# A graph network on one core: the first group of columns in two passes, with only the first part of its edges counted ahead

## Chip, cores, metric

The kernel runs on one core of a Trainium2 chip. The metric is device time in microseconds (us) of one execution; lower is better.

## The reference

A graph with N = 2500 nodes and E = 80000 edges, sorted by destination; 256 features; three layers.

```python
h = jnp.maximum(_layernorm(x), 0.0)
xs = [h]
for W, b in ((W0, b0), (W1, b1), (W2, b2)):        # W is 512 x 256
    xi, xj = h[dst], h[src]
    m = jnp.concatenate([xi, xj - xi], axis=-1) @ W + b
    s   = jax.ops.segment_sum(m, dst, num_segments=N)
    cnt = jax.ops.segment_sum(ones, dst, num_segments=N)
    h = jax.nn.relu(s / jnp.maximum(cnt, 1.0)[:, None])
    xs.append(h)
out = x + jnp.concatenate(xs, axis=-1) @ Wf + bf
```

The sum over a node's edges is a product with a matrix of counts: A[m, n] is the number of edges from m to n. Each layer multiplies node features (already times W) by A, and adds an "own" term from the node's features times its degree.

## The kernel before

**Names.** `P` = 128 partitions; `NT` = 20 tiles of 128 nodes; `DC` = 2 halves of the 256 features; `W` = 6 nodes in a window; `BW` = 4 windows in a block, which is 24 columns of A; `TURN` = 3 blocks. The columns of A are cut into 5 groups: four of 84 windows (504 columns, 21 blocks each) and one of 81 windows (486 columns). Blocks are numbered through: 0 to 20 are group 0, 21 to 41 group 1, and so on.

**Queues.** PE multiplies, DVE does elementwise work on one side, ACT on the other; POOL and SP mostly start transfers. The prefix `o` (`PEo`, `ACTo`, ...) means that instructions stay in the order in which the program writes them. Each engine takes its own in that order and waits on the others by semaphores. All such calls go through one helper, so they all have line 282 in the profile; there, they are told apart by tile names.

**Building A.** Three steps make a block b of A:

- `compare(b)`, on DVE: one-hot tiles `one_m` (source within its tile) and `one_n` (window position and tile). One call serves two blocks (15 with 16, 17 with 18, ...), except blocks 0 and 41, which stand alone. There are three buffers of each tile, so a compare waits until the blocks of three pairs earlier are counted.
- `counts(b)`, on PE: 8 small bf16 matmuls of `one_n` by `one_m` into a bank of PSUM.
- `take_counts(b, a)`, on ACT: a copy of that bank into the columns of tile `a` (20 tiles of rows by 504).

`build(g, a)` does this for a group in turns of three blocks and compares four blocks ahead. `degrees(i)` gets in-degrees: 8 sums on ACT (`junk`), three steps on DVE (`deg`, `deg_b`), four empty steps, then two sets of 6 small matmuls with a copy into `cnt`. `finish(g, a)` puts the degrees into a spare row of `a` and writes `a` out to `a_dram` in four transfers by POOL; for group 0, POOL's additions of x to `acc` follow.

**Head.** Normalizing x, finding edges, turning features, the products with W and Wf, and blocks of group 0 are woven together in an order written out by hand (the string `order`). In it, B is `compare`, C `counts`, E `take_counts`, with the block's number. Z and F are products (PE, tile `pz`, by W and by Wf, one pair q of tiles each); H and L split a Z product into a high and a low part (`zh` on ACT, `zl` on DVE); G copies an F product to `acc` on ACT. T and R turn features (PE, then ACT). `ws` is a subtraction on the own weights (`wt`) on DVE. The products have four banks of PSUM, and each is free for the next product, or after the head for something else, when H and L, or G, have read it. The head ends with all 21 blocks of group 0 counted and blocks up to 24 compared.

**Layer 0.** A loop goes over the five groups. `layer(l, g, a, own)` multiplies `zh` and `zl` with the group's columns, as a generator that yields after each unit. A unit is one row tile k: four matmuls (two feature halves, high and low) of 504 columns. Four further units are the own products (f32, tile `wt` by `hT`). After each unit the loop may step the next group's `build` (at the places in `at`) and an `extra` generator. For group 0, `extra` is

```python
extra = chain(degrees(0), finish(0, a), later_loads(), degrees(1))
```

stepped one and a half times a unit. `by_count(g)` multiplies `hT` with the degrees on DVE, ahead of the group's own units. So while group 0's columns are multiplied, group 1's blocks are counted.

**Rest.** Layers 1 and 2 read A back from `a_dram`, and use a fast form of the product on pairs of groups; the tail writes the result out.

Of the kernel before, what the change touches and what calls it, by code (L numbers as in the profile page):

```python
# [8 lines left out]
F32 = mybir.dt.float32  # L9
I32 = mybir.dt.int32  # L10
AF = mybir.ActivationFunctionType
# [296 lines left out]
def chain(*its):  # L308
    for it in its:
        yield from it  # L310
# [3 lines left out]
def by_windows(ctx: ExitStack, tc: tile.TileContext, x, src, dst, Ws, bs, Wf, bf, out, missing):  # L314
    nc = tc.nc
    PE, DVE, ACT, POOL, SP = nc.tensor, nc.vector, nc.scalar, nc.gpsimd, nc.sync
    PEo, DVEo, POOLo, ACTo, SPo = (InOrder(tc, e) for e in (PE, DVE, POOL, ACT, SP))
    P = 128
    N, D = x.shape
    E = src.shape[0]  # L320
    NT = (N + P - 1) // P
# [3 lines left out]
    DC = D // P  # L325
    R = E // P
    W = 6
# [10 lines left out]
    BW = 4  # L338
# [33 lines left out]
    def bank():  # L372
        return ps[-1].tile([P, 512], F32, name="bank")
# [10 lines left out]
    cnt = early.tile([P, NP], BF16, name="cnt")  # L384
# [29 lines left out]
    def tile_of(z, t):  # L414
        return z[:, t % 2, t // 2 * D:(t // 2 + 1) * D]
# [20 lines left out]
    ws = [None] * L  # L436
# [198 lines left out]
    def degrees(i):  # L635

        for q in range(W + 2):
            junk = hot.tile([P, CAP], BF16, name="junk2")
            ACTo.activation(junk, away[:, i, :], AF.Relu, bias=nc_[:, q:q + 1], accum_out=gsum[:, i, q:q + 1])
            yield  # L640
        DVEo.scalar_tensor_tensor(deg[:, i, :], gsum[:, i, 1:W + 1], -2.0, gsum[:, i, 0:W], op0=OP.mult, op1=OP.add)
        DVEo.tensor_add(deg[:, i, :], deg[:, i, :], gsum[:, i, 2:W + 2])
        DVEo.tensor_copy(deg_b[:, i, :], deg[:, i, :])
        yield
        yield
        yield
        yield
        for w0 in range(0, min(P, NW - i * P), P // 2):
            n = min(P // 2, NW - i * P - w0)
            pc = bank()  # L650
            for c in range(W):
                PEo.matmul(pc[:, :n * W].rearrange("p (w c) -> p w c", c=W)[:, :, c],
                          deg_b[:, i, c:c + 1].to_broadcast([P, P]), ident_b[:, w0:w0 + n], start=True, stop=True)
            to = (i * P + w0) * W
            ACTo.copy(cnt[:, to:to + n * W], pc[:, :n * W])
            yield
# [110 lines left out]
    def group_of(g):  # L767
        return sum(GWS[:g]) * W, GWS[g] * W
# [5 lines left out]
    def new_a(g):  # L774
        return apools[g % 2].tile([P, NT, GS], F32R, name="a")

    windows = [(g, s, min(BW, GWS[g] - s)) for g in range(NG) for s in range(0, GWS[g], BW)]
# [34 lines left out]
    def take_counts(b, a):  # L812
        _, s, nb = windows[b]
        ACTo.copy(
            a[:, :, s * W:(s + nb) * W].rearrange("p t (w c) -> p t w c", c=W),
            counted.pop(b)[:, :nb * NB].rearrange("p (w c t) -> p t w c", w=nb, c=W))

    def build(g, a):

        bs = [b for b in range(len(windows)) if windows[b][0] == g]  # L820
        for i in range(0, len(bs), TURN):
            for b in bs[i:i + TURN]:
                counts(b)
            for b in bs[i:i + TURN]:
                take_counts(b, a)
            for b in bs[i:i + TURN]:
                compare(b + AHEAD)
            yield

    def finish(g, a):  # L830
        c0, n = group_of(g)
        if n < GS:
            DVEo.memset(a[:, :, n:].bitcast(F32), 0.0)
        ACTo.copy(a[PAD:PAD + 1, NT - 1, :n], cnt[PAD:PAD + 1, c0:c0 + n])
        for t in range(0, NT, 5):
            POOLo.dma_start(a_dram[g][:, t:t + 5, :], a[:, t:t + 5, :].bitcast(F32))
        if g == 0:
            for t in range(0, NT, 5):
                add_x(t, t + 5)
        yield  # L840
# [6 lines left out]

    unit = [None]

    def layer(l, g, a, own, PE=PE, ACT=ACT):  # L850

        c0, n = group_of(g)
        pa = [ps_left.tile([P, 512], F32, name="bank") for _ in range(DC)]
        ways = [(o, c) for o in range(DC) for c in range(DC)]
        units = [(0, k) for k in BY_TURNS]
        for i, u in enumerate(own):
            units.insert(u + i, (1, i))
        last = {}
        for kind, i in units:
            last.update({o: (kind, i, o) for o in (range(DC) if kind == 0 else ways[i][:1])})  # L860
        for kind, i in units:
            if kind == 0:
                for o in range(DC):
                    for z in (zh, zl):
                        unit[0] = PE.matmul(pa[o][:, :n], tile_of(z, i)[:, o * P:(o + 1) * P], a[:, i, :n],
                                            start=(i == 0 and z is zh),
                                            stop=(z is zl and last[o] == (kind, i, o)))
            else:
                o, c = ways[i]
                unit[0] = PE.matmul(pa[o][:, :n], ws[l][0][:, c, o * P:(o + 1) * P], hT[:, c, c0:c0 + n],  # L870
                                    start=False, stop=(last[o] == (kind, i, o)))
            yield
        for o in range(DC):
            ACT.activation(hT[:, o, c0:c0 + n], pa[o][:, :n], AF.Relu)

# [3 lines left out]

    groups = [(0, 1), (1, 2), (2, 4), (4, 6), (6, 8), (8, Q)]
    a = new_a(0)
    acts = {
        "lim": limits, "first": find_first, "next": find_next, "pick": find_rows,
        "long": lengthen,
        "dstr": lambda: ACTo.copy(dst_r[:, MORE:], dst_i),
# [13 lines left out]
        long warm8 lim io first next dstr st0 rs0 sq0 pick sc0 warm7 N0 pk00 sg00 pk01 st1 T0 pk11 R0 sg01 st4 rs1 sq1 Z0 pk30 se0  # L901
        sg11 sc1 pk20 N1 st5 sg30 ge0 T1 st6 R1 rs3 F0 sg20 pk21 sq3 st7 pk10 H0 F1 rs4 st3 sq4 sc4 G0 st9
        sc3 L0 sg21 N6 pk31 ka0 kb0 Z1 N5 st8 N7 G1 T6 rs5 sg10 sg31 km0 T5 se1 kt0 R6 H1 st2 F6 sq5 sc5 k10 k20
        rs2 Z6 ge1 L1 T7 B0 R5 R7 Z5 B1 C0 B2 ka1 G6 H6 N9 H5 C1 T9 F7 E0 ge2 kb1 R9 sq2 km1 E1 kt1 C2 B3 k21 Z9
        k11 N8 L6 B4 E2 L5 C3 B5 C4 T8 E3 E4 C5 V9 R8 E5 ge3 ka2 H9 sc2 Z7 H7 F8 G7 B6 N3 N2 ka3 km2 T2 R2 km3
        kb2 C6 T3 kb3 B7 L7 kt2 Z2 B8 B9 L9 E6 C7 k22 k12 kt3 H2 N4 E7 B10 k13 k23 Z8 L2 C8 T4 C9 E8
        C10 H8 E9
        F9 B11 B12 C11 G8 E10 C12 R4 E12 E11 B13 F5 B14 C13 R3 B15 C14 E13 E14 L8 B16 Z3 G9 B17 C15 C16 H3 E15
        G5 B18 F3 C17 E16 C18 F4 E17 B19 C19 Z4 L3 G3 B20 E18 C20 B21 F2 E19 B22 H4 E20 L4 G4 B23 G2 B24 ws
    """  # L910

    def perform(order):
# [7 lines left out]
    ps_left = banks_of.enter_context(tc.tile_pool(name="ps_left", bufs=4, space=PSUM))  # L920
# [7 lines left out]
    def later_loads():  # L928
        load_wb(1, SPo)
        load_wt(1, SPo)  # L930
        load_wf(1, SPo)
        SPo.dma_start(bf_sb, bass.AP(tensor=bf.tensor, offset=bf.offset, ap=[[0, P], [1, D]]))
        yield
# [6 lines left out]
    E12 = 4096.0  # L940
    C1 = 1.0 + 1.0 / E12
# [61 lines left out]
            DVEo.tensor_add(acc[:, t:t + 5, :], acc[:, t:t + 5, :], bf_sb.unsqueeze(1).to_broadcast([P, 5, D]))  # L1003
            yield

    LATE = [NT] * 4
    extra = chain(degrees(0), finish(0, a), later_loads(), degrees(1))
    for g in range(NG):
        at = {}
        own = LATE  # L1010
        if g + 1 < NG:
            a1 = new_a(g + 1)
            one = build(g + 1, a1)
            left = -(-len([b for b in windows if b[0] == g + 1]) // TURN)
            units = NT + DC * DC
            at = {(i + 1) * (units - 1) // left - 1 for i in range(left)}
            if g:
                own = [u + 1 - i for i, u in enumerate(sorted(at)[1:5])]
        else:
            second.close()  # L1020
            ready = ctx.enter_context(tc.tile_pool(name="ready", bufs=7, side="right"))
            extra = chain(shares(), first_forms())
        for u, _ in enumerate(layer(0, g, a, own, PEo, ACTo)):
            if u in at:
                next(one)
            next(extra, None)
            if g == 0 and u % 2:
                next(extra, None)
            if g == 0 and u == NT // 2 + 3:
                by_count(0)  # L1030
            if u == NT - 1 and g + 1 < NG:
                run(extra)
                by_count(g + 1)
        run(extra)
        if g + 1 < NG:
            run(finish(g + 1, a1))
            a = a1
        extra = chain(degrees(g + 2) if g + 2 < WG else ())
# [261 lines left out]
    for l in range(1, L):  # L1300
# [7 lines left out]
        for i in range(Q + LAG):  # L1308
            if 0 < i <= Q:
                lone.make(i - 1)  # L1310
            if i < Q:
                q = order[i]
                n = Nodes(l, q)
# [51 lines left out]
    for i, q in enumerate(order):  # L1365
        po = bank()
        po = [po[:, :D], bank()[:, :D] if i == Q - 1 else po[:, D:]]
        for k in range(2):
            if q in PLAIN:
                for c in range(DC):  # L1370
                    PEo.matmul(po[k], hT[:, c, (2 * q + k) * P:(2 * q + k + 1) * P], wfs[L][:, c, :],
                               start=(c == 0), stop=(c == DC - 1))
            else:
                times(po[k], splits[q], k, coming[0])
        for k in range(2):
            t = 2 * q + k
            add_to_acc(t, po[k])
            n = P if t < NT - 1 else LAST
# [42 lines left out]
```

## Time and profile before

| | |
|---|---|
| median of 3 runs | 478.6 us (478.38 to 479.85) |
| profiled execution | 478.51 us |
| its span, first to last instruction | 476.7 us |
| mean granted TensorE clock | 0.996 |
| layer 0, group 0 on PE | 61.9 to 93.4 us of the span |
| PE busy / DVE busy / ACT busy | 465.9 / 375.0 / 302.1 us |

Times in the profile are counted from the span's start; the profiled execution takes 1.8 us more than its span. PE is the matmuls, PEld the loads of their weights. In a timeline, a row gives the start, the time, engine, line, operation, names out<-in, shapes and count, and in brackets the idle time ahead of it and what ended it. Consecutive instructions of a kind are merged. Ends of matmuls are modelled, so spacings are best taken from starts. The chain of waits is followed back from the last instruction to whatever released each one.

### The profile page before, as it was taken

To read this page: it belongs to the slowest core of one execution; us is meant where nothing else is said; L and a number is where in the kernel's file an instruction comes from. 1 tells how busy PE (TensorE), PEld (TensorE's weight loads), DVE (VectorE), ACT (ScalarE), POOL (GpSimd) and SP (SyncE) were. 2 spreads that over 40 slices of the span, in tenths; PEclk is the share of its full clock that TensorE was granted. 3 is DMA by queue.
4 is the path that set the end of the run, shared out by engine and by line. 5 is a ranking of instruction groups with operands and counts; after the bars stand their busy time and mean duration, and the time that the engine had idled before them with its cause. 6 is when DMAs were issued, how large, how long until landed. Compare 5 with 4: busy or idle time off the path is not lost.

```text
span 476.7 us, 7301 instructions
## 1 busy us (share of the span) xinstructions
PE 465.9 (98%) x2723; PEld 366.5 (77%) x2723; DVE 375.0 (79%) x687; ACT 302.1 (63%) x527; POOL 41.6 (9%) x66
## 2 busy tenths in 40 slices
PE   7999999999999999999999999999999999999994
PEld 4887888777777778878887877876788788688694
DVE  8988987987788874649987847877899687569785
ACT  5776576664554435067778866874787798497540
POOL 3681015200100101000000000000000000000000
PEclk9999999999999999999999999999999999999998
DMA  9310078990550905522268551110213955220033
GB/s 285 112 53 4 1 156 162 192 214 9 102 118 1 203 16 101 119 89 52 79 188 321 210 174 27 61 43 2 87 43 90 356 185 175 87 88 0 0 98 124
DMA packets 21845, 52.73 MB, mean 111 GB/s; under 512 B 1977, under 2 KB 12170, under 8 KB 21770
## 3 DMA queue, kind: packets, MB, share of 16 engines
q1 hardware_dynamic: 14730, 34.31, 21.2%
q0 software_dynamic: 5856, 16.51, 18.2%
q10 hardware_dynamic: 1216, 1.37, 0.9%
q8 instruction: 23, 0.38, 0.3%
q14 instruction: 20, 0.16, 0.1%
HBM read 36.72 MB, written 16.10 MB: 111 GB/s over the span
## 4 chain that ended last, share of the span: by engine, by line
PE 87%; DVE 7%; DMA 2%; POOL 2%; issue 1%; SPq 0%; DVEq 0%
PE bank L282 85%; PE pz L282 2%; DMA acc<-in_x_dram 1%; DVE st L282 1%; DVE acc L282 1%; POOL acc L282 1%; DVE one_m L282 1%; DVE staged L282 1%; DMA es<-longer,start_i 1%; POOL ed L282 1%; DVE one_n L282 1%; DVE zl L282 0%; DVE away L282 0%; DVE mv L282 0%; POOL es L282 0%
## 5 line engine op out<-in xcount | busy, mean ns | idle before, releaser
L282 ACT CAST block<-staged 128x1008 fp32r<-128x1008 bf16 x120 | 117.8, 1031 | 16.9 <-DVE staged L282 6.3
L282 ACT CAST a<-bank 128x480 fp32r<-128x480 f32 (+1 forms) x105 | 52.9, 565 | 60.7 <-PE bank L282 60.7
L282 PE MATMUL bank<-a,zh 128*128 128x504 f32 (+1 forms) x200 | 84.4, 422 | 0.0
L282 PE MATMUL bank<-block,zh 128*128 128x504 f32 (+1 forms) x200 | 83.8, 419 | 0.0
L282 DVE TENSOR_TENSOR one_m<-iota_m,key_m 128x2048 bf16<-128x2048 bf16 (+2 forms) x55 | 64.3, 1169 | 21.4 <-PE bank L282 21.3
L282 PE MATMUL bank<-a,zl 128*128 128x504 f32 (+1 forms) x200 | 77.9, 389 | 0.0
L282 PE MATMUL bank<-block,zl 128*128 128x504 f32 (+1 forms) x200 | 77.4, 387 | 0.0
L282 PE MATMUL bank<-block,sh 128*128 128x504 f32 x160 | 69.1, 432 | 0.0
L282 PE MATMUL bank<-block,staged 128*128 128x512 f32 (+1 forms) x312 | 66.5, 365 | 0.3 <-DVE staged L282 0.3
L282 PE MATMUL bank<-block,sl 128*128 128x504 f32 x160 | 62.7, 392 | 0.0
L282 PEld LDWEIGHTS bank<-block,staged 128*128 128x128 f32 x312 | 52.5, 188 | 10.7 <-issue 0.7
L282 DVE TENSOR_TENSOR one_n<-iota_n,key_n 128x960 bf16<-128x960 bf16 (+2 forms) x110 | 55.5, 545 | 0.0
L282 DVE TENSOR_TENSOR block<-staged 128x1008 fp32r<-128x1008 bf16 x40 | 46.9, 1205 | 5.5 <-PE bank L282 4.3
L282 PEld LDWEIGHTS <-one_m 128*128 128x128 bf16 x834 | 39.1, 98 | 11.2 <-issue 7.2
L282 PEld LDWEIGHTS bank<-a,zh 128*128 128x128 f32 x200 | 37.8, 189 | 10.7 <-issue 2.6
L282 PEld LDWEIGHTS bank<-block,zh 128*128 128x128 f32 x200 | 37.6, 188 | 10.8 <-issue 2.5
L282 PEld LDWEIGHTS bank<-block,zl 128*128 128x128 f32 x200 | 37.6, 188 | 10.5 <-issue 3.2
L282 PE MATMUL bank<-one_n,one_m 128*128 128x120 bf16 x834 | 44.5, 209 | 1.1 <-DVE one_n L282 1.0
L282 PEld LDWEIGHTS bank<-a,zl 128*128 128x128 f32 x200 | 37.8, 189 | 8.9 <-issue 2.6
L282 DVE TENSOR_TENSOR staged<-staged 128x1008 bf16<-128x1008 bf16 x40 | 27.1, 679 | 17.3 <-ACT block L282 16.9
L282 PE MATMUL pz<-wbf,hT 128*128 128x256 f32 x160 | 38.6, 387 | 0.7 <-DMA wbf<-in_L_gnn_Wf_dram 0.4
L282 PEld LDWEIGHTS bank<-block,sh 128*128 128x128 f32 x160 | 30.1, 188 | 10.4 <-issue 3.5
(155 smaller groups left out, 591.1 us busy)
## 6 DMA issues: line engine op xcount, KB each, us to landing
staged<-a_dram SPq DMA_DIRECT2D x52, 504.0 KB, 4.0
a_dram<-a POOLq DMA_DIRECT2D x20, 630.0 KB, 8.6
out_dram<-acc SPq DMA_DIRECT2D x17, 128.0 KB, 1.8
acc<-in_x_dram POOLq DMA_DIRECT2D x3, 640.0 KB, 13.1
wbf<-in_L_gnn_Wf_dram SPq DMA_DIRECT2D x4, 256.0 KB, 6.9
acc<-in_x_dram SPq DMA_DIRECT2D x1, 896.0 KB, 9.4
acc<-in_x_dram ACTq DMA_DIRECT2D x1, 768.0 KB, 6.9
wbf<-in_L_gnn_W_dram SPq DMA_DIRECT2D x3, 256.0 KB
```

Source lines behind the costliest of these rows:

```text
L282: return self.tc.keep_in_program_order(call(*args, **kwargs))
```

## The change

Group 0 is multiplied in two passes: first its columns 0 to 263 (blocks 0 to 10), then columns 264 to 503 (blocks 11 to 20).

- The head counts blocks 0 to 10 only, and compares up to 14. Ten counts, ten copies and five pairs of compares leave it. Ten steps of `degrees(0)` come into it (D in the order): the 8 sums on ACT, the DVE steps, one empty step.
- `layer` takes `cuts`. With one cut it has two spans, each with its own two banks of PSUM (four in all), its own 80 matmuls (264 or 240 columns) and its own pair of final activations.
- During the first pass, after units 0, 5, 10 and 15, blocks 11 to 20 are counted, copied and the next ones compared. During the second pass, after units 20, 23, 26, 30, 33, 36 and 40, group 1's blocks are.
- The own units of the first span stand in the second pass (from unit 28), those of the second at its end. There are thus 8 of half the width instead of 4.
- `extra` is stepped once a unit. The first span's part of the degree row is written in the first pass, the rest and the transfers of `finish` after unit 20.

```diff
+    def with_degrees(a, c0, x0, x1):
+        ACTo.copy(a[PAD:PAD + 1, NT - 1, x0:x1], cnt[PAD:PAD + 1, c0 + x0:c0 + x1])
     def finish(g, a):
...
-        ACTo.copy(a[PAD:PAD + 1, NT - 1, :n], cnt[PAD:PAD + 1, c0:c0 + n])
+        with_degrees(a, c0, 0 if g else HALF * BW * W, n)
...
-    def layer(l, g, a, own, PE=PE, ACT=ACT):
+    def layer(l, g, a, own, PE=PE, ACT=ACT, cuts=()):
         c0, n = group_of(g)
-        pa = [ps_left.tile([P, 512], F32, name="bank") for _ in range(DC)]
+        ends = [0, *cuts, n]
+        spans = list(zip(ends, ends[1:]))
+        pa = {(s, o): ps_left.tile([P, 512], F32, name="bank")[:, :s[1] - s[0]] for s in spans for o in range(DC)}
         ways = [(o, c) for o in range(DC) for c in range(DC)]
-        units = [(0, k) for k in BY_TURNS]
-        for i, u in enumerate(own):
-            units.insert(u + i, (1, i))
+        units = [(s, k, None) for s in spans for k in BY_TURNS]
+        for i, (u, s) in enumerate(own):
+            units.insert(u + i, (spans[s], None, ways[i % len(ways)]))
...
-                        unit[0] = PE.matmul(pa[o][:, :n], tile_of(z, i)[:, o * P:(o + 1) * P], a[:, i, :n],
+                        unit[0] = PE.matmul(pa[s, o], tile_of(z, k)[:, o * P:(o + 1) * P], a[:, k, s[0]:s[1]],
...
+            if ending[s] == (k, way):
+                for o in range(DC):
+                    ACT.activation(hT[:, o, c0 + s[0]:c0 + s[1]], pa[s, o], AF.Relu)
             yield
...
-        C10 H8 E9
-        F9 B11 B12 C11 G8 E10 C12 R4 E12 E11 B13 F5 B14 C13 R3 B15 C14 E13 E14 L8 B16 Z3 G9 B17 C15 C16 H3 E15
-        G5 B18 F3 C17 E16 C18 F4 E17 B19 C19 Z4 L3 G3 B20 E18 C20 B21 F2 E19 B22 H4 E20 L4 G4 B23 G2 B24 ws
+        C10 H8 E9
+        F9 B11 D B12 G8 E10 R4 B13 F5 B14 R3 L8 Z3 G9 H3 D
+        G5 F3 F4 Z4 L3 G3 F2 H4 L4 G4 G2 ws
...
-    LATE = [NT] * 4
-    extra = chain(degrees(0), finish(0, a), later_loads(), degrees(1))
+    def second_half(a):
+        yield from build(0, a, HALF)
+        built.append(0)
+    def when_built():
+        with_degrees(a, 0, 0, HALF * BW * W)
+        while not built:
+            yield
+    HALF = 11
+    extra = chain(early_degrees, when_built(), finish(0, a), later_loads(), degrees(1))
...
+        passes = 1 if g else 2
+        own = [(NT + 8, 0)] * 4 + [(NT * 2, 1)] * 4 if g == 0 else [(NT, 0)] * 4
...
+            if g == 0:
+                one = chain(second_half(a), one)
+                at = {0, 5, 10, 15} | {NT + u - 2 for u in at}
...
-        for u, _ in enumerate(layer(0, g, a, own, PEo, ACTo)):
+        for u, _ in enumerate(layer(0, g, a, own, PEo, ACTo, () if g else (HALF * BW * W,))):
             if u in at:
                 next(one)
             next(extra, None)
-            if g == 0 and u % 2:
-                next(extra, None)
-            if g == 0 and u == NT // 2 + 3:
+            if g == 0 and u == NT + 2:
                 by_count(0)
-            if u == NT - 1 and g + 1 < NG:
+            if u == NT * passes - 1 and g + 1 < NG:
                 run(extra)
                 by_count(g + 1)
```

More of the change, by code (lines that the diff above doesn't have):

```diff
@@ L816, in take_counts, with build @@
             counted.pop(b)[:, :nb * NB].rearrange("p (w c t) -> p t w c", w=nb, c=W))
-    def build(g, a):
-        bs = [b for b in range(len(windows)) if windows[b][0] == g]
+    def build(g, a, start=0):
+        bs = [b for b in range(len(windows)) if windows[b][0] == g][start:]
         for i in range(0, len(bs), TURN):
@@ L858, in layer @@
         last = {}
[L859 to L862, printed above, removed]
+        ending = {}
+        for s, k, way in units:
+            ending[s] = k, way
+            last.update({(s, o): (k, way) for o in (range(DC) if way is None else way[:1])})
+        for s, k, way in units:
+            if way is None:
                 for o in range(DC):
                     for z in (zh, zl):
-                        unit[0] = PE.matmul(pa[o][:, :n], tile_of(z, i)[:, o * P:(o + 1) * P], a[:, i, :n],
-                                            start=(i == 0 and z is zh),
-                                            stop=(z is zl and last[o] == (kind, i, o)))
-            else:
-                o, c = ways[i]
-                unit[0] = PE.matmul(pa[o][:, :n], ws[l][0][:, c, o * P:(o + 1) * P], hT[:, c, c0:c0 + n],
-                                    start=False, stop=(last[o] == (kind, i, o)))
+                        unit[0] = PE.matmul(pa[s, o], tile_of(z, k)[:, o * P:(o + 1) * P], a[:, k, s[0]:s[1]],
+                                            start=(k == 0 and z is zh), stop=(z is zl and last[s, o] == (k, None)))
+            else:
+                o, c = way
+                unit[0] = PE.matmul(pa[s, o], ws[l][0][:, c, o * P:(o + 1) * P], hT[:, c, c0 + s[0]:c0 + s[1]],
+                                    start=False, stop=(last[s, o] == (None, way)))
+            if ending[s] == (k, way):
+                for o in range(DC):
+                    ACT.activation(hT[:, o, c0 + s[0]:c0 + s[1]], pa[s, o], AF.Relu)
@@ L872, in layer @@
             yield
-        for o in range(DC):
-            ACT.activation(hT[:, o, c0:c0 + n], pa[o][:, :n], AF.Relu)
     groups = [(0, 1), (1, 2), (2, 4), (4, 6), (6, 8), (8, Q)]
     a = new_a(0)
+    early_degrees = degrees(0)
     acts = {
+        "D": lambda: next(early_degrees),
         "lim": limits, "first": find_first, "next": find_next, "pick": find_rows,
@@ L903, in by_windows @@
         sc3 L0 sg21 N6 pk31 ka0 kb0 Z1 N5 st8 N7 G1 T6 rs5 sg10 sg31 km0 T5 se1 kt0 R6 H1 st2 F6 sq5 sc5 k10 k20
-        rs2 Z6 ge1 L1 T7 B0 R5 R7 Z5 B1 C0 B2 ka1 G6 H6 N9 H5 C1 T9 F7 E0 ge2 kb1 R9 sq2 km1 E1 kt1 C2 B3 k21 Z9
-        k11 N8 L6 B4 E2 L5 C3 B5 C4 T8 E3 E4 C5 V9 R8 E5 ge3 ka2 H9 sc2 Z7 H7 F8 G7 B6 N3 N2 ka3 km2 T2 R2 km3
-        kb2 C6 T3 kb3 B7 L7 kt2 Z2 B8 B9 L9 E6 C7 k22 k12 kt3 H2 N4 E7 B10 k13 k23 Z8 L2 C8 T4 C9 E8
+        rs2 Z6 ge1 L1 T7 B0 R5 R7 Z5 B1 C0 B2 ka1 G6 H6 N9 H5 C1 T9 F7 E0 D ge2 kb1 R9 sq2 km1 E1 D kt1 C2 B3 k21 Z9
+        k11 N8 L6 B4 E2 D L5 C3 B5 C4 T8 E3 D E4 C5 V9 R8 E5 D ge3 ka2 H9 sc2 Z7 H7 F8 G7 B6 N3 N2 ka3 km2 T2 R2 km3
+        kb2 C6 T3 kb3 B7 L7 kt2 Z2 B8 B9 L9 E6 D C7 k22 k12 kt3 H2 N4 E7 D B10 k13 k23 Z8 L2 C8 T4 C9 E8 D
         C10 H8 E9
-        F9 B11 B12 C11 G8 E10 C12 R4 E12 E11 B13 F5 B14 C13 R3 B15 C14 E13 E14 L8 B16 Z3 G9 B17 C15 C16 H3 E15
-        G5 B18 F3 C17 E16 C18 F4 E17 B19 C19 Z4 L3 G3 B20 E18 C20 B21 F2 E19 B22 H4 E20 L4 G4 B23 G2 B24 ws
+        F9 B11 D B12 G8 E10 R4 B13 F5 B14 R3 L8 Z3 G9 H3 D
+        G5 F3 F4 Z4 L3 G3 F2 H4 L4 G4 G2 ws
     """
@@ L1004, in first_forms @@
             yield
-    LATE = [NT] * 4
-    extra = chain(degrees(0), finish(0, a), later_loads(), degrees(1))
+    built = []
+    def second_half(a):
[7 more added lines that the diff above has]
+    extra = chain(early_degrees, when_built(), finish(0, a), later_loads(), degrees(1))
     for g in range(NG):
         at = {}
-        own = LATE
+        passes = 1 if g else 2
+        own = [(NT + 8, 0)] * 4 + [(NT * 2, 1)] * 4 if g == 0 else [(NT, 0)] * 4
         if g + 1 < NG:
@@ L1016, in by_windows @@
             at = {(i + 1) * (units - 1) // left - 1 for i in range(left)}
+            if g == 0:
+                one = chain(second_half(a), one)
+                at = {0, 5, 10, 15} | {NT + u - 2 for u in at}
             if g:
-                own = [u + 1 - i for i, u in enumerate(sorted(at)[1:5])]
+                own = [(u + 1 - i, 0) for i, u in enumerate(sorted(at)[1:5])]
         else:
```

## The prediction

> **What bounds the kernel now.** I read the page first, then the chain of waits, then the stretches around the end of the head, then timelines. The page gives the engine, the chain says from when on.
>
> ```profile
> PE 465.9 (98%) x2723; PEld 366.5 (77%) x2723; DVE 375.0 (79%) x687; ACT 302.1 (63%) x527; POOL 41.6 (9%) x66
> PE 87%; DVE 7%; DMA 2%; POOL 2%; issue 1%; SPq 0%; DVEq 0%
> ```
>
> ```profile
> 47.26 0.49 DVE one_n L282
> 47.75 0.04 issue
> 47.80 0.81 PE bank L282 x15
> 48.61 1.80 PE pz L282 x8
> 50.41 0.71 PE bank L282 x16
> ...
> 60.45 1.80 PE pz L282 x8
> 62.25 400.54 PE bank L282 x2258
> ```
>
> The last piece of the chain that is not PE's, until the tail, is a compare ending at 47.75 us: block 11 waits for its one_n. From there PE is the chain for 415 us. So the stretch from which the change takes work (47.5 to 61.9) and the one into which it puts work (61.9 to 93.4, layer 0 of group 0) have the same bound:
>
> ```profile
> core 0: us, PE busy (x) PEld busy (x) DVE busy (x) ACT busy (x) POOL busy (x), PEclk, DMA share, GB/s
> 47.48:61.90 14.42, 14.32 (x129) 12.55 (x129) 13.14 (x20) 8.84 (x18) 0.42 (x1) 1.00 0.01 1
> 61.90:93.37 31.47, 31.47 (x283) 24.49 (x281) 26.89 (x46) 21.32 (x60) 8.69 (x9) 1.00 1.00 181
> ```
>
> A busy PE may hide slack, so I checked by start times: between 47.48 and 61.90 stand ten count blocks of 0.355 us (3.55) and six products of 1.80 (10.8), 14.35 in all. It is full except for block 11's wait, 0.26 us.
>
> **What the Trainium skill says.** "TensorE: Matmul & The Clock Gate", Back-to-back issue gap: the isolated gap is N/2.4 + 2.5 ns, and in a stream the weight load also sets the spacing. Halving a matmul would thus cost some 2.5 ns each. The trace spaces 504 columns by 0.228 us, above the formula's 212 ns; I use the trace. Same page, LDWEIGHTS: 128 columns take about P/1.2, 107 ns, whatever the row count. A 240-column matmul at 1/2.4 ns per column is 100 ns, so its load is barely covered. The trace has the nearest case in its tail (256 columns, new weights each time, 119 ns). "VectorE: DVE Perf Modes", perf-mode tier table: a bf16 tensor_tensor of 2048 takes 1224 ns; one_m takes 1.22 us here, so compares have nothing to gain. "Perfetto Trace Analysis", Identifying the Most-Contended Engine: matmul busy share is a bad measure of headroom; hence the sums by start times.
>
> **The prices**, in the PE timeline:
>
> ```profile
> 64.37 0.40 PE L282 MATMUL bank<-a,zh 128*128 128x504 f32 x1
> 64.60 0.39 PE L282 MATMUL bank<-a,zl 128*128 128x504 f32 x1
> 64.84 1.24 PE L282 MATMUL bank<-one_n,one_m 128*128 128x120 bf16 x24
> 65.90 0.48 PE L282 MATMUL bank<-a,zh 128*128 128x504 f32 x1
> 66.22 0.39 PE L282 MATMUL bank<-a,zl 128*128 128x504 f32 x1
> ...
> 455.18 5.87 PE L282 MATMUL bank<-block,staged 128*128 128x256 f32 x48
> 460.89 0.38 PE L282 MATMUL bank<-wbf,hT 128*128 128x256 f32 x1
> ```
>
> Read starts, not durations: 64.60 - 64.37 gives 0.228 us for 504 columns; a turn of three blocks takes 1.06; the first matmul after a turn takes 0.32, 0.09 over the rest. The 256-column run is (460.89 - 455.18)/48 = 0.119 us. A line through 0.228 and 0.119 has 0.44 ns a column and 6 ns fixed.
>
> **The change, step by step (PE).**
> 1. Removed from the head: blocks 11 to 20. By starts they take 0.97 (11, 12, with the wait) + 3 x 0.71 + 2 x 0.355 = **-3.81 us**. The six products among them stay, now back to back.
> 2. Added in the first pass: the same ten blocks, 10 x 0.355 = **+3.55**, in four turns, each followed by the slower first matmul, 4 x 0.09 = **+0.36**.
> 3. 80 matmuls of 504 columns become 160 of 264 and 240: 80 x 6 ns = **+0.5**. Bounds: -1.4 if one column costs 1/2.4 ns and nothing else (160 x 105 against 80 x 228 ns), +1.4 if the whole 18 ns over 210 is fixed. The middle is the trace's own 256-column row. The 8 own passes in f32 become 16 of half width; 256 columns take 0.225 and 504 take 0.445, so nothing.
> 4. A new wait. Block 11's bank now comes from the banks that the head's products held, one unit (0.49 us) into the layer, and in the changed program its matmul waits for the copy of the last product F2 (G2 on ACT). Before, no block came until three units were done.
>
> ```profile
> 62.29 0.59 ACT L282 COPY acc<-pz 128x512 f32<-128x512 f32 x1 [0.62 <-PE pz L282]
> ```
>
> That copy ends 0.98 us after the layer's first matmul; block 11 would start at 0.49. **+0.45** (0 to 0.6). Behind it in PE's order stands the whole first pass.
>
> **The change on DVE.** Five pairs of blocks (15/16 to 23/24) leave the head: 5 x 2.11 us (starts 64.06, 66.17) = 10.6. They aren't free time gained: DVE then waits in the head for L8, L3, L4, which follow the products, and can't run ahead, since the pairs stand behind L4 and "ws" in its order.
>
> ```profile
> 60.75 0.69 DVE L282 TENSOR_TENSOR zl<-pz,zh 128x512 fp32r<-128x512 f32 x1 [1.28 <-ACT zh L282]
> 63.46 0.68 DVE L282 TENSOR_TENSOR wt<-wt,wbf 128x512 f32<-128x512 f32 x1
> 64.06 1.22 DVE L282 TENSOR_TENSOR one_m<-iota_m,key_m 128x2048 bf16<-128x2048 bf16 x1
> ...
> 69.30 1.23 DVE L282 TENSOR_TENSOR one_m<-iota_m,key_m 128x2048 bf16<-128x2048 bf16 x1 [0.94 <-PE bank L282]
> ...
> 78.72 1.23 DVE L282 TENSOR_TENSOR one_m<-iota_m,key_m 128x2048 bf16<-128x2048 bf16 x1 [2.47 <-PE bank L282]
> 80.83 1.27 DVE L282 TENSOR_TENSOR hT<-hT,cnt 128x504 f32<-128x504 f32 x2
> ```
>
> Those gaps at 69.30 and 78.72 (and 0.89 at 92.19) are all the slack DVE had in the layer: 31.47 - 26.89 = 4.6 us. I laid both orders side by side from the layer's start T. DVE: L4 ends at T - 0.35, "ws" at T + 0.3, then pairs of 2.11, each held until the blocks of three pairs earlier are counted. Pair 15 ends at 2.4, 17 at 4.5, 19 at 7.9 (waits for block 14), 21 at 10, 23 at 12, 25 at 15.1 (block 20), 27 at 18.3 (block 22); then by_count(0), 1.2; 29 at 21.6; 31 at 23.7; 33 at 25.8; 35 at 27.9; deg 0.55; 37 at 30.6; 39 at 32.7; 41 (single, 1.1) at 33.8. PE, with steps 2 to 4, asks for block 19 at 9.7, 25 at 18.2, 29 at 21.1 (**0.5 late**), 31 at 24.2, 33 at 26.4, 35 at 27.1 (**0.8 late**), 37 at 30.9, 39 at 33.5, 41 at 34.2. So **+1.3** of DVE waits in the second pass (0 to 3: each margin is under 1.5 us, and one late pair delays all behind it).
>
> **What else moves.** Eight degree sums go to the head, 8 x 0.5 on ACT. ACT idles 6 us between 31 and 45, the sums follow E's, and the queue is caught up at H7 (35.55) and H2 (41.06): nothing for PE. After E8 it runs 0.5 late; H8, G8, R4, R3 have 0.7 or more before their products. The three deg steps on DVE push pair 13 and L8 by 0.5: L8 ends at about 50.95 and F3, which takes that bank, starts at 51.08. Nothing, but tight (0 to 0.3). POOL's 4 a_dram writes and the additions of x, and SP's four later loads, keep their order and are issued at T + 17 = 75 us, against 76.7 before: nothing, since group 2's first copy comes 20 us later. Four accumulation banks instead of two: the first pass's are emptied in the second, before group 1 needs them: nothing. In group 1 DVE is ahead again (block 42 asked 4 us after its pair).
>
> **Sum.** -3.81 + 3.55 + 0.36 + 0.5 + 0.45 + 1.3 = **+2.3 us**. Head ends at about 58.1, group 0's layer at 95.7 instead of 93.4. Profiled execution 478.51 (span 476.7 and 1.8 around it), 0.1 under the median 478.6; so 480.8 against the former, and **480.9** as a median. About 0.3% (1.4 us) can be told from no change.
>
> **Rivals.**
> - A. As summed, PE work moved and small waits added: 479.8 to 482.6. For it: a full PE on both sides. Chance 0.62.
> - B. DVE becomes the bound of group 0's layer. 13 pairs, one single, 42/43, both by_counts and deg are 34 us, plus 2.9 of buffer waits, in a layer PE needs 36 for; should each of the last eight pairs come 0.4 later (say, a late "ws"), +3.2: 484. Chance 0.15.
> - C. The change costs PE only its sums (no late pair, no bank wait): +0.6, 479.2. For it: margins that I may have taken too tight. Chance 0.15.
> - D. Faster: PE takes short matmuls and their loads without overhead. A column costs 1/2.4 ns and nothing else (-1.4 in step 3), the slower first matmul after a turn is gone (step 2 at 3.55), and no wait comes: -3.81 + 3.55 - 1.4 = -1.7, 476.9. It decides once a 264-column matmul is spaced under some 113 ns; the 256-column row (119) speaks against it. Chance 0.08. That the head's DVE-bound part gets shorter is excluded: all that PE waits for before block 11 (0.38 at 32.85, 0.35 at 38.96, 0.30 at 41.33) stays where it is.
>
> Range 478.8 to 484.0: it leaves out most of D, the edge of C and the far end of B. Faster 0.07 (D), same 0.18 (C and A's lower edge), slower 0.75.
>
> **What the changed profile would show.** Layer 0's first 264-column matmul at 58.1 (58 to 58.6). Spacing of 264 and 240 columns: 0.122 and 0.112 us. PE idle at block 11 put down to ACT's acc copy. Blocks 29 and 35 waiting for one_n. DVE with 10 us more in that layer and gaps of a few us in the head. First matmul of group 1 at 95.7. I am wrong if group 1 starts before 93 us, or if PE shows no wait in the second pass.

## The result, and the profile after

The change makes the kernel slower by about 2 us: 480.73 us (median of 6 runs, 480.34 to 481.79) against 478.8 for the kernel before (6 runs, 478.38 to 479.85), ratio 1.0041 [1.0031, 1.0052]. The profiled execution took 480.81 us, with a span of 479.0 us at a granted clock of 0.996. The forecast was 480.9.

The busy line of the changed kernel's page, and the shares of its chain by engine:

```profile
PE 466.7 (97%) x2811; PEld 372.7 (78%) x2811; DVE 374.8 (78%) x687; ACT 302.5 (63%) x530; POOL 41.6 (9%) x66
PE 86%; DVE 7%; DMA 3%; POOL 2%; issue 1%; ACT 0%; SPq 0%; DVEq 0%
```

There are 88 more matmuls (80 from the two passes, 8 from the own units). PE is busy 0.8 us longer in a span 2.3 us longer, so most of the loss is not work. The chain of waits shows where PE no longer carries it:

```profile
45.81 12.39 PE pz L282 x56
...
58.23 0.59 ACT acc L282
...
58.87 15.23 PE bank L282 x188
...
79.53 1.22 DVE one_m L282
...
83.82 1.14 DVE one_m L282
84.96 0.98 DVE one_n L282 x2
...
85.98 378.92 PE bank L282 x2093
```

Before, PE was the chain from 47.80 us on. Now an ACT copy stands in it at 58.23, and DVE's one-hots stand in it in the second pass. The same stretches as before, cut at the new end of the head:

```profile
core 0: us, PE busy (x) PEld busy (x) DVE busy (x) ACT busy (x) POOL busy (x), PEclk, DMA share, GB/s
45.65:57.84 12.19, 12.19 (x60) 10.47 (x58) 6.58 (x13) 6.16 (x13) 0.00 (x0) 1.00 0.00 0
57.84:95.41 37.57, 36.45 (x451) 34.82 (x449) 34.54 (x54) 23.27 (x57) 10.47 (x12) 1.00 0.75 138
```

The head ends 4.06 us earlier than before (57.84 against 61.90). The layer takes 37.57 us instead of 31.47, which is 6.10 more. So group 1 starts 2.04 us later (95.41 against 93.37), and that is nearly all of the 2.3 us in the span. In the layer, PE stands idle 1.12 us between its instructions; before, it showed no idle time there. DVE is busy 34.5 us of 37.6, where it was 26.9 of 31.5. PE's timeline in the layer (start, time, engine, line, operation, count, and in brackets the idle time ahead and what ended it):

```profile
57.84 0.47 PE L282 MATMUL bank<-a,zh 128*128 128x264 f32 x1
...
58.87 1.22 PE L282 MATMUL bank<-one_n,one_m 128*128 128x120 bf16 x24 [0.19 <-ACT acc L282]
...
70.94 0.28 PE L282 MATMUL bank<-a,zl 128*128 128x264 f32 x1
...
72.63 0.28 PE L282 MATMUL bank<-a,zl 128*128 128x264 f32 x1
...
74.46 0.28 PE L282 MATMUL bank<-a,zl 128*128 128x240 f32 x1
...
75.58 0.28 PE L282 MATMUL bank<-a,zl 128*128 128x240 f32 x1
...
79.27 0.23 PE L282 MATMUL bank<-one_n,one_m 128*128 128x120 bf16 x1 [0.19 <-DVE one_n L282]
79.66 0.46 PE L282 MATMUL bank<-one_n,one_m 128*128 128x80 bf16 x7 [0.17 <-DVE one_n L282]
...
85.58 0.23 PE L282 MATMUL bank<-one_n,one_m 128*128 128x120 bf16 x1 [0.41 <-DVE one_n L282]
85.98 0.46 PE L282 MATMUL bank<-one_n,one_m 128*128 128x80 bf16 x7 [0.17 <-DVE one_n L282]
...
95.41 0.57 PE L282 MATMUL bank<-a,zh 128*128 128x504 f32 x1
```

Starts tell more than the brackets, since the modelled end of the matmul ahead covers part of each wait. Against the spacing without a wait, block 11 starts 0.35 us late, block 29 (79.27 and 79.66) is late by 0.69 and block 35 by 0.90, together **1.94 us**. From 70.94 to 72.63 are 14 matmuls of 264 columns, 0.121 us each; from 74.46 to 75.58 ten of 240, 0.112 each. And DVE in the same layer:

```profile
57.12 0.69 DVE L282 TENSOR_TENSOR zl<-pz,zh 128x512 fp32r<-128x512 f32 x1 [4.71 <-ACT zh L282]
...
63.80 1.23 DVE L282 TENSOR_TENSOR one_m<-iota_m,key_m 128x2048 bf16<-128x2048 bf16 x1 [1.17 <-PE bank L282]
...
70.95 1.22 DVE L282 TENSOR_TENSOR one_m<-iota_m,key_m 128x2048 bf16<-128x2048 bf16 x1 [0.74 <-PE bank L282]
...
74.12 1.23 DVE L282 TENSOR_TENSOR one_m<-iota_m,key_m 128x2048 bf16<-128x2048 bf16 x1 [0.98 <-PE bank L282]
...
76.23 1.27 DVE L282 TENSOR_TENSOR hT<-hT,cnt 128x504 f32<-128x504 f32 x2
```

DVE has nothing to do for 4.71 us at the end of the head. It then waits 2.89 us for free buffers: 1.91 in the first pass, and 0.98 at the start of the second, which begins at 72.75. Then it does `by_count(0)` (76.23) ahead of the one-hots that PE needs next. Up to 74.12 DVE waits for PE; from 78.9 on PE waits for DVE.

### The profile page after: what moved, and what is told of

It reads as the page before. It is cut to its first block, busy times and chain, and to the rows that moved or that the text cites. A ratio compares the mean times of both kernels' runs of the same rounds, so it can differ in the third digit from the quotient of the medians.

```text
span 479.0 us, 7483 instructions
## 1 busy us (share of the span) xinstructions
PE 466.7 (97%) x2811; PEld 372.7 (78%) x2811; DVE 374.8 (78%) x687; ACT 302.5 (63%) x530; POOL 41.6 (9%) x66
## 4 chain that ended last, share of the span: by engine, by line
PE 86%; DVE 7%; DMA 3%; POOL 2%; issue 1%; ACT 0%; SPq 0%; DVEq 0%
PE bank L282 83%; PE pz L282 3%; DMA acc<-in_x_dram 1%; DVE one_m L282 1%; DVE one_n L282 1%; DVE acc L282 1%; DMA es<-in_src_dram,start_i 1%; POOL acc L282 1%; DVE staged L282 1%; POOL ed L282 1%; DMA es<-longer,start_i 1%; DVE st L282 1%; POOL es L282 0%; DVE away L282 0%; DVE kn L282 0%
## 5 line engine op out<-in xcount | busy, mean ns | idle before, releaser
L282 PE MATMUL bank<-a,zh 128*128 128x504 f32 (+3 forms) x240 | 89.0, 383 | 0.0
L282 PE MATMUL bank<-a,zl 128*128 128x504 f32 (+3 forms) x240 | 81.6, 352 | 0.0
L282 PEld LDWEIGHTS bank<-a,zh 128*128 128x128 f32 x240 | 45.4, 189 | 8.7 <-issue 2.6
L282 PEld LDWEIGHTS bank<-a,zl 128*128 128x128 f32 x240 | 45.3, 189 | 7.7 <-issue 2.6
L282 PEld LDWEIGHTS bank<-block,zh 128*128 128x128 f32 x200 | 37.6, 188 | 10.8 <-issue 2.5
L282 PEld LDWEIGHTS bank<-block,zl 128*128 128x128 f32 x200 | 37.6, 188 | 10.6 <-issue 3.2
L282 PE MATMUL pz<-wbf,hT 128*128 128x256 f32 x160 | 37.4, 384 | 0.8 <-DMA wbf<-in_L_gnn_Wf_dram 0.5
```

What stands on the lines that cost most here:

```text
L282: return self.tc.keep_in_program_order(call(*args, **kwargs))
```

## Experiments

All ratios are to the kernel before, run beside each experiment on the same chip (478.56, 478.79 and 478.91 us in the three sets of runs). The head in the order of before ended at 61.64, 61.90, 62.02 and 62.16 us in four traces, so a single start is read to about 0.5 us, and lengths within a stretch more finely. The head of the changed kernel ended at 57.84 to 57.87 in four traces. From group 1's first matmul to the end of the span the traces take 383.3 to 384.4 us, except for that of `two_passes_five_groups`, which changes the later groups too; so the spans of two single traces say little below 1 us. Medians and the layer's own length say more.

### The split of the matmuls alone

`two_passes_alone` is the kernel before with only the layer of group 0 in two passes. All 21 blocks are still counted in the head, and group 1's turns stand at the doubled places. The basis of the three kernels of this part, on the changed one:

```diff
-    HALF = 11
+    HALF, CUT = 21, 264
...
-    extra = chain(early_degrees, when_built(), finish(0, a), later_loads(), degrees(1))
+    extra = chain(degrees(0), when_built(), finish(0, a), later_loads(), degrees(1))
...
-                at = {0, 5, 10, 15} | {NT + u - 2 for u in at}
+                at = {2 * u for u in at}
```

and the order of the head is that of the kernel before (`CUT` also takes the place of the old cut where the degree row is written and where `layer` is called).

> The head is that of before (all 21 blocks counted, compares up to 24); only layer 0 of group 0 runs in two passes of 264 and 240 columns, group 1's turns spread over both. Theory A (the forecast's sum: PE is full on both sides, so the moved blocks cancel and what is left is the price of short matmuls, turns and new waits): PE pays only the split, 0.4 us by the changed kernel's spacings (80 x 0.1207 + 80 x 0.1117 against 80 x 0.228): 0.1 to 0.8 us over before, PE without a wait in the layer. Rival S (the split itself is the whole loss, for instance by loads of weights that are no longer covered): 1.5 to 2.5 us over before.

Measured: 479.49 us, ratio 1.0018 [1.0010, 1.0025], +0.9 us. The layer runs from 61.64 to 93.78, 32.14 us, +0.67 on the kernel before. Two causes stand out. The spacings give 80 x (0.121 + 0.112 - 0.228) = +0.4. The other is one wait, in which the degree matmuls of group 1 come before DVE has their sums (idle before them in PE's timeline):

```profile
81.40 0.51 PE L282 MATMUL bank<-ident_b,deg_b 128*128 128x64 bf16 x6 [0.27 <-DVE deg_b L282]
```

The bracket has 0.27 us; by starts this matmul is 0.44 late (0.66 after the one ahead, where 0.22 is usual), so the other small changes of order give back some 0.2. The split itself is what theory A said, and the expectation missed a wait that the rearrangement brought. The rival's 18 ns for each matmul is out.

`two_passes_five_groups` does the same for all five groups (`passes = 2`, the cut passed for each).

> As two_passes_alone, but all five groups of layer 0 run in two passes (264 and 240 columns; the last 264 and 222). It multiplies the price of the split by five. Theory A: 5 x 0.4 to 0.5 = 2.0 to 2.5 us over before. Rival S: 7 us or more. If a bank of PSUM is waited for at the change of groups, PE shows it as a wait for ACT.

Measured: 481.46 us, ratio 1.0059 [1.0045, 1.0073], +2.8 us. That is above A's range and far under the rival's. The reason is the last group: its 486 columns become 264 and 222, and the 222 are spaced by 0.111 us (29 spacings from 196.30 to 199.53 us), hardly less than 240. That group would pay 80 x (0.121 + 0.111 - 0.222) = +0.8 by the spacings, and is 1.3 us longer in the trace (22.82 us to the first matmul of layer 1, against 21.56). Groups 1 to 3 are 0.36, 0.31 and 0.33 longer, and the first 0.67, with the same wait for `deg_b`: 2.9 in all. What makes the last group dearer than its spacings was not separated.

`uneven_cut` cuts at 384 instead of 264 columns.

> As two_passes_alone with the cut at column 384: 80 matmuls of 384 columns and 80 of 120. Theory A's line (0.44 ns a column and 6 ns fixed) gives 0.175 and 0.059 us and the same 0.5 us over before. If a load of weights takes the 107 ns that the Trainium skill states (TensorE: Matmul & The Clock Gate, LDWEIGHTS) and can't be hidden by a shorter matmul, 120 columns are spaced by 0.107 us: 80 x (0.175 + 0.107 - 0.228) = 4.3 us over before. I expect the latter, 3.5 to 5.

Measured: 484.2 us, ratio 1.0120 [1.0105, 1.0136], +5.7 us. Its PE timeline gives both spacings:

```profile
67.03 0.34 PE L282 MATMUL bank<-a,zl 128*128 128x384 f32 x1
...
70.89 0.34 PE L282 MATMUL bank<-a,zl 128*128 128x384 f32 x1
...
80.64 0.28 PE L282 MATMUL bank<-a,zh 128*128 128x120 f32 x1
...
82.53 0.28 PE L282 MATMUL bank<-a,zl 128*128 128x120 f32 x1
```

From 67.03 to 70.89 are 22 spacings of 0.175 us; from 80.64 to 82.53 are 17 of 0.111. So 120 columns are spaced like 222 and nearly like 240: there is a floor. The Trainium skill, "TensorE: Matmul & The Clock Gate", LDWEIGHTS, puts the load of 128 columns of weights at 107 ns; the trace's 111 is close to that, as would be if the load sets the pace, but these runs don't vary the load, so its part is not shown. A load's own record lasts 0.19 us in this trace, longer than the page's 107 ns; the records overlap, and in the stretch of 120 columns one begins every 0.111 us. The split costs 80 x (0.175 + 0.111 - 0.228) = +4.7 here. The layer is longer by 5.15 (36.62 us, 62.02 to 98.64): besides these 4.7, the own products take 4.12 us by their starts where they took 3.65. Many of them stand between other matmuls here, and where pieces of 120 columns follow one another they too are 0.111 us apart. The expectation took the load's 0.107 and left the own products out, and its upper end was too low.

### The degrees' sums

`sums_back` takes the ten D steps out of the changed kernel's head, so that they run in the layer.

> The changed kernel with the ten steps of degrees(0) back in the layer (units 0 to 13, one a unit). It asks whether the sums on ACT in the head cost something that the forecast put at nothing. Theory A: they cost nothing there, so 480.7, within 0.5 us of the changed kernel, and the layer starts at 57.8 as there. Rival H (ACT's sums hold up the head): the layer starts 0.5 us or more earlier, and the time is 0.5 to 1 us lower.

Measured: 480.94 us, ratio 1.0045 [1.0031, 1.0059], by time the same as the changed kernel. The layer takes 37.56 us (57.36 to 94.92) against 37.57. But it starts 0.48 us earlier, where A said 57.8: nearly H's start, without H's time. The starts of the seven products show what the D steps cost. In the changed kernel their matmuls follow one another by 0.216 us, but for the first after the blocks and these two (PE, then DVE's L8):

```profile
50.69 0.38 PE L282 MATMUL pz<-wbf,hT 128*128 128x256 f32 x1
51.02 0.48 PE L282 MATMUL pz<-wbf,hT 128*128 128x256 f32 x1
...
50.28 0.69 DVE L282 TENSOR_TENSOR zl<-pz,zh 128x512 fp32r<-128x512 f32 x1
```

The matmul at 51.02 is the first of F3, which takes the bank that L8 (50.28) empties. It comes 0.33 us after the one ahead, just after L8's end at 50.97, and the next one 0.32 after it: **0.22 us** late in all. The brackets don't show it, since the modelled end of the matmul ahead covers it. `late_turn`, `early_count` and `spread`, with the same D steps in the head, have 0.21 to 0.22 at the same place. In `sums_back` L8 stands 0.53 us earlier in its sequence, since the three steps on DVE are gone from ahead of it, and F3 isn't late. The other 0.26 us is gained at 38.79 (39.05 in the changed kernel), where PE's wait for DVE's `kn` is missing from this one trace. The kernel before, which has no D steps in its head either, has that wait, so the wait isn't put down to them. So the degree steps in the head cost 0.22 us at F3, which the time does not resolve.

### The waits of the layer, one by one

`late_turn` puts the first turn of the first pass one unit later.

```diff
-                at = {0, 5, 10, 15} | {NT + u - 2 for u in at}
+                at = {1, 5, 10, 15} | {NT + u - 2 for u in at}
```

> The changed kernel with the first turn of the first pass after its second unit instead of its first (turns at units 1, 5, 10 and 15). Theory A (each of the layer's waits is a time on the path of its own): block 11 no longer comes before ACT has copied the last of the head's banks, so its 0.35 us goes; nothing else moves. 0.3 us less than the changed kernel: 480.4 us. Group 1 starts at about 95.1. Rival: PE's time is given by the engines ahead of it, so the wait turns up at the next turn; 480.7.

Measured: 480.6 us, ratio 1.0039 [1.0026, 1.0052]. By time alone this can't be told from the changed kernel. By the trace it is what A said: the wait for ACT's `acc` is gone, blocks 29 and 35 are late by 0.7 and 0.9 as in the changed kernel, and group 1 starts at 95.09 after a layer that began at 57.85 (37.24 us, 0.33 less).

`early_count` moves `by_count(0)` on DVE from the second pass into the first.

```diff
-            if g == 0 and u == NT + 2:
+            if g == 0 and u == 4:
                 by_count(0)
```

> The changed kernel with by_count(0) (VectorE's work of 1.2 us that the count of edges needs) called in unit 4 of the first pass instead of in unit 2 of the second: VectorE then does it where it waits for a free buffer of one-hots. Theory A (blocks 29 and 35 are late because VectorE makes the one-hots just in time behind this work): block 29's 0.69 us goes and block 35's 0.90 is about halved. About 1.1 us less than the changed kernel: 479.6, still above the kernel before (478.6 to 478.8). Rival (these waits hide behind something else): no change, 480.7.

Measured: 479.54 us, ratio 1.0018 [1.0011, 1.0025], 1.2 us less than the changed kernel. Group 1 starts at 94.27, 1.14 earlier. The waits of PE in the layer (engine, tile, releaser: us in total, times, longest), first of the changed kernel:

```profile
PE bank L282 <- DVE one_n L282: 0.9, 4, 0.4
PE bank L282 <- ACT acc L282: 0.2, 1, 0.2
```

and then of this one:

```profile
PE bank L282 <- ACT acc L282: 0.2, 1, 0.2
PE bank L282 <- DVE one_n L282: 0.2, 1, 0.2
```

By starts, block 29 isn't late any more and block 35 is by 0.45, half of what it was, as A said. A piece of 1.2 us on an engine that looks 92% busy in the layer cost 1.1 us more in one place than in the other.

`spread` adds to that a more even place for all eleven turns.

```diff
-                at = {0, 5, 10, 15} | {NT + u - 2 for u in at}
+                at = {1, 5, 9, 13, 18, 22, 26, 30, 33, 36, 40}
```

> The changed kernel with by_count(0) in unit 4 and the eleven turns of blocks spread over both passes (units 1, 5, 9, 13, 18, 22, 26, 30, 33, 36, 40). Theory A: all three waits of TensorE in the layer (1.94 us) go, and what is left of the change is the head's saving of 4.06, ten blocks at 3.55, their four turns at 0.36 and the split of the matmuls at 0.38: +0.2 us over the kernel before, 478.8 to 479.2. Rival (VectorE is the bound of the layer, so waits come back elsewhere): 480 or more. If it comes out more than 0.3% under the kernel before (under 477.3), theory A falls, since something other than the waits was paid.

Measured: 478.91 us, ratio 1.0005 [0.9998, 1.0011]: the time of the kernel before. The busy time by stretch:

```profile
45.70:57.87 12.17, 12.17 (x61) 10.46 (x57) 6.57 (x13) 6.15 (x13) 0.00 (x0) 1.00 0.00 0
57.87:93.54 35.67, 35.67 (x450) 34.58 (x449) 34.52 (x54) 23.07 (x57) 10.46 (x12) 1.00 0.76 142
```

PE shows no idle time in the layer any more (by starts block 35 is still late by 0.14), with the same matmuls as the changed kernel and DVE as busy as there (34.5 us). 35.67 is 1.90 less than 37.57: this is nearly the 1.94 of waits. The work that was moved, the slower matmuls after a turn and the split give 31.47 + 3.55 + 0.36 + 0.38 = 35.76. So it was not the amount of DVE's work that made PE wait in this layer, but its order and the places at which PE asks for it. And with these waits gone, two passes only draw level.

### PE's waits ahead of block 11

Neither kernel touches the waits that PE has in the head before 47.5 us. `fill` is the kernel before with the hand order rewritten there: Z7 ahead of C5; L9, `kb2` and L7 into DVE's gap at 34.6 to 36.9 us; C6 ahead of T2; Z2 ahead of `kt2`; Z8 ahead of C7; F9 and F5 earlier.

```diff
-        k11 N8 L6 B4 E2 L5 C3 B5 C4 T8 E3 E4 C5 V9 R8 E5 ge3 ka2 H9 sc2 Z7 H7 F8 G7 B6 N3 N2 ka3 km2 T2 R2 km3
-        kb2 C6 T3 kb3 B7 L7 kt2 Z2 B8 B9 L9 E6 C7 k22 k12 kt3 H2 N4 E7 B10 k13 k23 Z8 L2 C8 T4 C9 E8
+        k11 N8 L6 B4 E2 L5 C3 B5 C4 T8 E3 E4 V9 R8 Z7 C5 ge3 ka2 H9 sc2 L9 E5 kb2 H7 F8 G7 B6 N3 N2 L7 C6 ka3 km2 T2 R2 km3
+        T3 E6 kb3 B7 Z2 kt2 B8 B9 Z8 C7 k22 k12 kt3 H2 N4 E7 B10 k13 k23 G8 L2 T4 C8 H8 E8 F9 C9 C10 E9
...
-        F9 B11 B12 C11 G8 E10 C12 R4 E12 E11 B13 F5 B14 C13 R3 B15 C14 E13 E14 L8 B16 Z3 G9 B17 C15 C16 H3 E15
+        B11 B12 F5 C11 E10 C12 R4 E12 E11 B13 B14 C13 R3 B15 C14 E13 E14 L8 B16 Z3 G9 B17 C15 C16 H3 E15
```

> The kernel before, its first group in one pass, with another hand-written order of the head: the small steps that TensorE and ACT and VectorE can do at once (the norm products Z7, Z2, Z8, the products L9 and L7, the copies F9, F5) stand ahead of the compares of edges and the counts that are not ready. Theory: in the head TensorE stands idle for 2.2 us in all between 20 and 47.5 us, at the counts C5 (0.9), at the norm's products (0.5) and at C7 (0.8), and work put there takes most of it: about 1.9 us less than the kernel before, 476.9. Rival: the waits only move, since the edges' loads or VectorE's compares set when C5 and C7 can start: 478.6 to 478.8.

Measured: 478.7 us, ratio 1.0001 [0.9993, 1.0009]. The time is that of the rival, but the reason is another: the waits at C5 and C7 are gone from PE's timeline, and after block 10 PE has at 46.21 us what it had at 47.48 in the profile before, 1.3 us ahead. Block 11's wait (0.26) is gone too. Then this comes:

```profile
48.01 0.87 PE L282 MATMUL bank<-one_n,one_m 128*128 128x120 bf16 x16
49.53 0.97 PE L282 MATMUL bank<-one_n,one_m 128*128 128x120 bf16 x16 [0.65 <-ACT a L282]
```

With F5 taken away from behind block 12, four count blocks follow one another, and the third must wait until ACT has emptied a bank. By starts the four blocks take 2.48 us (48.01 to 50.49) where 1.41 would do, so 1.07 us were given back, more than the bracket's 0.65, and the layer starts at 61.47, 0.43 ahead of the profile before. The time does not show that much.

`fill_banks` mends that: R3 and Z3 come ahead of F3's place, and a product stands between each two pairs of blocks again.

```diff
-        B11 B12 F5 C11 E10 C12 R4 E12 E11 B13 B14 C13 R3 B15 C14 E13 E14 L8 B16 Z3 G9 B17 C15 C16 H3 E15
-        G5 B18 F3 C17 E16 C18 F4 E17 B19 C19 Z4 L3 G3 B20 E18 C20 B21 F2 E19 B22 H4 E20 L4 G4 B23 G2 B24 ws
+        B11 B12 F5 C11 E10 C12 R3 E12 E11 B13 Z3 B14 L8 C13 R4 B15 C14 E13 E14 B16 F3 G9 H3 B17 C15 C16 E15
+        G5 L3 B18 F4 C17 E16 C18 Z4 E17 G3 B19 C19 B20 E18 C20 B21 F2 E19 B22 H4 E20 L4 G4 B23 G2 B24 ws
```

> The kernel before, one pass, with the hand order of fill and one thing more: the products R3 and Z3 stand ahead of F3, so that a product again stands between each two pairs of count blocks. In fill PE was 1.0 us ahead of the kernel before when blocks 9 and 10 were counted, and 0.65 us of that went to four count blocks in a row on two banks (idle before the third put to ACT's copy a). Theory: with that wait away, layer 0 starts at about 60.8 us instead of 61.5 to 61.9, and the time is 0.9 to 1.3 us under the kernel before: 477.5 to 477.9. Rival (the waits of the head only move, whatever the order): within 0.3 us of the kernel before.

Measured: 477.3 us, ratio 0.9965 [0.9953, 0.9977]: faster than both kernels, by 1.6 us against the one before, and more than the 0.9 to 1.3 expected, which took the wait at its bracket. In its PE timeline the wait is a product now:

```profile
47.97 0.87 PE L282 MATMUL bank<-one_n,one_m 128*128 128x120 bf16 x16
48.67 1.97 PE L282 MATMUL pz<-wbf,hT 128*128 128x256 f32 x8
...
60.33 0.58 PE L282 MATMUL bank<-a,zh 128*128 128x504 f32 x1
```

The layer starts at 60.33, 1.57 us earlier than in the profile before (1.3 by block 10, and block 11's 0.26), and takes 31.46 us, as there (to 91.79).

`spread_fill` puts the order of `fill` for the head into `spread`.

> The kernel spread (two passes, by_count(0) early, eleven spread turns) with the head's order of fill, which there has no four blocks in a row. Theory A (moving the blocks is a zero sum; what can still be had in the head is PE's waits ahead of block 11, and both kernels have the same): 1.0 us less than spread, 477.9, and so no better than fill_banks. Rival: with VectorE's pairs out of the head the two-pass kernel takes the early products better, and comes out under fill_banks by 0.5 us or more.

Measured: 478.13 us, ratio 0.9987 [0.9978, 0.9995]. It gains 0.8 us on `spread` by the two medians (1.0 expected) and is 0.8 us above `fill_banks`. Its layer takes 35.70 us (56.48 to 92.18), `spread`'s 35.67. By the traces its head gains 1.39 us on `spread`'s, `fill_banks`'s 1.57 on that of before. So most of the gain in the head is had with and without two passes, and two passes add nothing to it; why the medians differ by 0.4 us more than group 1's starts (92.18 and 91.79) was not traced.

## Why the prediction was right

The end of the layer was put at 95.7 and came at 95.41; the time at 480.9 and came at 480.73. The layer's start, put at 58.1 (58 to 58.6), came at 57.84, just outside. The mechanism is the one forecast: work moved from one stretch in which PE is full to another, so it gained next to nothing, and new waits for ACT and DVE came on top. By the steps:

1. **Blocks out of the head** (-3.81): 45.68 to 61.90 became 45.65 to 57.84, -4.03. The direction and nearly all of the size are right. Two errors of opposite sign are in it. A product's first matmul takes 0.29 us to the next one after blocks, and 0.22 in a row of products, so a product costs 1.80 or 1.73; six of them lost their blocks, which is -0.46. Step 2 charges such a slower first matmul after each turn, but step 1 did not take it off. And F3's wait for L8 gave 0.22 back.
2. **Blocks and turns in the first pass** (+3.55 and +0.36): borne out as a sum by `spread`, whose layer, all but free of waits, is 35.67 us where the terms give 35.76. They were not measured one by one.
3. **The split** (+0.5): +0.4 by the spacings of 0.121 and 0.112 (forecast 0.122 and 0.112), and `two_passes_alone` leaves 0.2 to 0.4 when its one wait is taken off. The bounds of -1.4 and +1.4 are both excluded. But the line through 504 and 256 columns holds only down to about 240: `uneven_cut` shows the floor under it, and at 240 the cut stands right at that floor. By the prediction's own figures, 100 ns for 240 columns against 107 for a load, the load was not "barely covered" but not covered. That the line fits at 240 is luck: the cut at 384 cost 4.7 us by its spacings, where the line gives 0.5.
4. **Block 11 and G2's copy** (+0.45): +0.35, by ACT's `acc` as said; `late_turn` takes it away and the layer is 0.33 shorter. The copy ended 0.97 us into the layer (0.98 forecast). The block was due only at 0.67, not 0.49, since the layer's first matmul took 0.31 us.
5. **DVE** (+1.3): blocks 29 and 35, the two that were named, are late by 0.69 (0.5 forecast) and 0.90 (0.8). Laying out DVE's order by hand gave pairs 25, 27 and 35 ending at 15.1, 18.3 and 27.9 after the layer's start; they ended at 15.3, 18.5 and 28.1. `early_count` and `spread` show that these waits were paid: 1.14 us go in the first, and 1.90, block 11's among them, in the second. DVE has 7.7 us more to do in the layer, not 10: in the kernel before, most of the pair at 61.36 and half of the one at 92.19 fell into the layer too, and one set of degree steps has left it.
6. **Costed at nothing**: the degree steps in the head. L8 ended at 50.97 and F3 was due at 50.91, so this cost 0.22, within the 0 to 0.3 that the prediction allowed it. The sums on ACT show no cost of their own. POOL, SP and the four banks show no wait of PE's in the layer; they were not tried by themselves.

That the sum came so close is partly luck. Steps 1, 3 and 4 came out 0.4 us under their forecasts together and step 5 0.3 over, and they nearly cancel; -4.03 + 3.55 + 0.36 + 0.4 + 0.35 + 1.59 = +2.2 stands beside 2.04 at the end of the layer. The remaining 0.3 us of the span come after the layer (383.6 us against 383.3) and were not traced to a place; the traces differ there by up to 1.1 us.

Of the rivals, B (DVE as the bound) is refuted by `spread`: DVE has as much to do there, and PE shows no idle time. C (only the sums) describes `spread`, not the changed kernel. D (short matmuls without overhead) needed a 264-column spacing under 113 ns; it is 121.

## To carry to other kernels

Work that was moved from one stretch in which an engine is full to another in which the same engine is full gained nothing here; ask first whether the two have different bounds, and look for the idle time that is left (here PE's waits in the head, worth 1.6 us) instead. When an engine that feeds the bound loses its lead, the order of its work can matter more than its load: write out, for the few instructions that the bound waits for, when each is ready and when it is asked for, and move what isn't needed yet into the producer's own waits. And when work is pulled ahead of a wait, check that what it separated (here pairs of blocks on two banks) is still separated. Read a wait from the spacing of starts too: the bracket held 0.65 of 1.07 us once, and nothing of 0.22 another time.

## What the runs showed of the hardware

In a stream of the layer's matmuls (zh or zl with a), each with its own weights of 128 columns, the spacing is 0.228 us at 504 columns, 0.175 at 384, 0.121 at 264 and 0.112 at 240, but still 0.111 at 222 and at 120: cutting below about 240 columns brings nothing. Pieces of 120 columns of the own products are 0.111 us apart too. The bf16 matmuls of the counts, also with their own weights each, are 0.053 us apart at 120 columns, so the floor is not one of all types. A product of eight matmuls takes 1.80 us after blocks of bf16 and 1.73 in a row of its kind; the 0.08 us lie at its first matmul, and what in the switch costs them was not separated.
